# Padding rows dropped at the scatter, scatters of one expert made independent, and the last batch's routing woven in differently

## The chip, the cores and the metric

The kernel runs on one core of a Trainium2 chip. The metric is the device time of one execution in microseconds; the median of three timed runs is given. The core has five engines that run side by side, each in its own order: PE (matrix products), DVE (vectors), ACT (activation functions and copies), POOL (further element-wise work, and here all indirect DMAs), and SP (which here only issues DMAs). They wait for one another through semaphores. DMAs move data between device memory and the on-chip memory.

## The reference, cut to what matters

Two layers act on 4 x 32 x 32 positions of 256 channels, which are 4096 tokens in 4 batches. Layer 0 is a convolution with a state-space scan; layer 1 is an attention and then a mixture of 16 experts. The change concerns the experts:

```python
logits = jnp.einsum('bsd,de->bse', x, gate_w) + gate_b
probs = jax.nn.softmax(logits, axis=-1)
top_probs, top_idx = jax.lax.top_k(probs, 2)
top_probs = top_probs / jnp.sum(top_probs, axis=-1, keepdims=True)
dispatch = jnp.sum(jax.nn.one_hot(top_idx, n_experts, dtype=x.dtype) * top_probs[..., None], axis=-2)
h1 = jnp.einsum('bsd,edh->bseh', x, w1)
h2 = jnp.einsum('bsd,edh->bseh', x, w2)
hidden = jax.nn.silu(h1) * h2
expert_out = jnp.einsum('bseh,eho->bseo', hidden, w3)
return jnp.einsum('bseo,bse->bso', expert_out, dispatch)
```

Every token goes to two of 16 experts, and the two weighted results are added to the token's row `t`, which holds the attention's output. There are 8192 (token, expert) pairs. The input of the experts is the layer-normalised row.

## The kernel before, in words

**Stages.** The scan of layer 0 fills the first 2690 us. The attention of the four batches follows (loop `for o in range(NB)`, line 1817), with the routing of batch `z = o - 1` woven into that of batch `o`. Then comes the expert stage (`blocks_of`, line 2091). The order within an engine is that of the program text (`tc.manual_schedule()`).

**Blocks.** The pairs are sorted by expert into blocks of `BS` = 128 rows. Each expert has `FIX` = 3 fixed blocks; number `s * NE + e` is the s-th of expert e. Pairs that don't fit go to extra blocks, whose expert is known only at run time: `NFULL` = 25 of them always run, further ones only under `tc.If`. That makes 8 + 40 + 25 = 73 blocks: `soon` are the first blocks of experts 0 to 7 (filled from batches 0 to 2 alone), `fixed` are the other 40 fixed ones, and `more` the 25 extra ones.

**One block.** `fetch_rows` (1801) gathers 128 rows of `xd`, the normalised tokens in DRAM, by an indirect DMA on POOL's queue (`src` holds the row numbers, `xb` the rows). `turn_rows` (2037) transposes them on PE into `px`, and ACT copies that to `xT`. `hidden` (2054), called twice a block, forms half of both hidden products on PE (`p12`), the silu on ACT (`s`) and the product on DVE (`hT`). `result` (2073) multiplies by `w3` on PE into `pf`. `put_result` (2082) weighs the result on DVE (`yb`, four buffers) and adds it to the output by an indirect DMA on POOL's queue:

```python
        nc.gpsimd.indirect_dma_start(
            of[:, :], bass.IndirectOffsetOnAxis(dst[:, c : c + 1], 0), yb, None,
            compute_op=ALU.add,
        )
```

All these scatters write the same DRAM tensor, so each waits for the one before it to land.

**Padding.** A block that isn't full has padding rows. They gather the zero row 4096 of `xd`, and add zeros to rows of `out`. [...]padding is sent to tokens that are not in the block. `nonmembers`, `count_them`, `place_them` and `list_them` (1664 to 1696) list 128 such tokens per expert (`table`); `one_block` and `targets` (1770 to 1784), and the end of `more_rows` (2241 to 2270), turn it into the target rows `dst`.

**Order of the stage.** `blocks_of` walks the list `todo`. In step i it gathers ahead (`look_ahead`: four blocks beyond i, six `xb` buffers), computes the first half of block i, the second half of the result of block i - 1 with its scatter, loads weights ahead (`load_ahead`, on SP's queue), transposes block i + 1, and computes the second half of block i. `more` blocks are spread one by one among the fixed ones. Weights of fixed and extra blocks live in separate pairs of buffers (`wp` and `spare`; the names in the profile are `w` and `m`).

**Routing of the last batch.** The routing of batch 3 and the lists of the later blocks depend on the end of the attention. They are a generator (`rest_of_routing`, `spare_rows`, `more_places`, `more_rows`), cut by `yield` into steps. `on_with(beside, 3)` runs three steps after each half block while i < 8, and one step after that. PE steps among them: `turn_e` (transposes), `gates` (gate product), `turn_g`, the counts `pc` (1574), the lists `pf_r` (1652), the extra blocks' experts (2183) and lists (2228).

Of the kernel before, what the change touches and what calls it, by code (L numbers as in the profile page):

```python
# [33 lines left out]
def conv_ssm_attn_moe_kernel(ctx: ExitStack, tc: tile.TileContext, a: dict, out: bass.AP):  # L34
# [1149 lines left out]
    names = l1.tile([P, 2], F32, name="names")  # L1184
    names_h = l1.tile([P, 2], BF16, name="names_h")
    apart = l1.tile([P, 2, NE], F32, name="apart")
    rank = l1.tile([P, 2, NE], F32, name="rank")
    table = l1.tile([P, NE], F32, name="table")
# [17 lines left out]
    def constants(first):  # L1206
# [6 lines left out]
        if first:  # L1213
# [8 lines left out]
            count(names, 2, 0, P, 1)  # L1222
            count(part_pk, 2, 1, 1, 2)
            count(block_p, 1, 0, 1, 1)
        else:
# [8 lines left out]
            nc.vector.tensor_copy(names_h, names)  # L1234
# [293 lines left out]
    def route(b):  # L1528
# [42 lines left out]
        yield  # L1571
        flat = hot2.rearrange("p e g -> p (e g)")
# [60 lines left out]
        nc.vector.tensor_tensor(  # L1633
# [15 lines left out]
        pf = ps_c.tile([P, 2, NFIX], F32, name="pf_r", tag="po")  # L1649
        for k in range(2):  # L1650
            for i in range(NT):
                nc.tensor.matmul(
                    pf.rearrange("p s n -> p (s n)"), qh[:, k, b * NT + i, :],
                    code[:, k * NT + i, :2, :].rearrange("p s n -> p (s n)"),
                    start=(k + i == 0), stop=(k == 1 and i == NT - 1),
                )
# [7 lines left out]
    def nonmembers():  # L1664
        nc.gpsimd.tensor_tensor(apart, hot_all[:, 0, :2, :], hot_all[:, 1, :2, :], ALU.add)
        nc.gpsimd.tensor_scalar(apart, apart, -1.0, 1.0, ALU.mult, ALU.add)

    def count_them():
        pa = ps_c.tile([P, 2, NE], F32, name="pa", tag="po")
        nc.tensor.matmul(pa[:, 0, :], before, apart[:, 0, :], start=True, stop=True)  # L1670
        nc.tensor.matmul(pa[:, 1, :], before, apart[:, 1, :], start=True, stop=False)
        nc.tensor.matmul(pa[:, 1, :], every, apart[:, 0, :], start=False, stop=True)
        nc.scalar.copy(rank, pa)

    def place_them():
        nc.gpsimd.tensor_scalar(apart, apart, -4.0 * P, 4.0 * P, ALU.mult, ALU.add)
        nc.gpsimd.tensor_tensor(rank, rank, apart, ALU.add)
        at = batch[0]["at"] = att.tile(
            [P, 2, NE, BS], BF16, name="at_rank", tag="xh", bufs=2
        )  # L1680
        for g in range(2):
            for e in range(NE):
                nc.gpsimd.tensor_scalar(  # L1683
                    at[:, g, e, :], places_f, rank[:, g, e : e + 1], 1.0,
                    ALU.is_equal, ALU.mult,
                )

    def list_them():
        pt = ps_c.tile([P, NE], F32, name="pt_r", tag="po")
        for e in range(NE):  # L1690
            for g in range(2):
                nc.tensor.matmul(
                    pt[:, e : e + 1], batch[0]["at"][:, g, e, :], names_h[:, g : g + 1],
                    start=(g == 0), stop=(g == 1),
                )
        nc.scalar.copy(table, pt)

    def on_with(steps, n):
        for _ in range(n):
            next(steps, None)  # L1700
# [33 lines left out]
    dst = late.tile([P, NBLK], I32, name="dst")  # L1734
# [6 lines left out]
    move = late.tile([P, NBLK], F32, name="move")  # L1741
    other = late.tile([P, NE], F32, name="other")
    full = late.tile([P, NE], F32, name="full")
# [26 lines left out]
    def targets(lo, hi, move):  # L1770

        cs = slice(lo, hi)
        nc.vector.scalar_tensor_tensor(
            move, move, -1.0 * NB * L, none[:, cs], ALU.add, ALU.mult
        )
        nc.vector.tensor_tensor(dst[:, cs], token[:, cs], move, ALU.add)

    def one_block(lo, hi, held):

        cs = slice(lo, hi)  # L1780
        nc.vector.tensor_scalar(full[:, cs], held[:, cs], float(BS), None, ALU.is_ge)
        nc.vector.tensor_tensor(other[:, cs], token[:, cs], table[:, cs], ALU.subtract)
        nc.vector.tensor_tensor(other[:, cs], other[:, cs], full[:, cs], ALU.mult)
        nc.vector.tensor_tensor(other[:, cs], other[:, cs], table[:, cs], ALU.add)

# [3 lines left out]
    weights = {}  # L1789

# [10 lines left out]
    def fetch_rows(key):  # L1801
# [3 lines left out]
        if c < 3:  # L1805
            t = sm.tile(
                [P, C + 2], F32, name="xb_s", tag="qk" if c else "junk", bufs=2 if c else 1
            )
        else:
            t = on_b["ffn"].tile([P, C + 2], F32, name="xb", bufs=6)  # L1810
# [6 lines left out]
    for o in range(NB):  # L1817
# [26 lines left out]
        if o == 2:  # L1844
            nonmembers()
        if o == 3:
            place_them()
            first_weights("w1")
            first_weights("w3")
        v_out(o, 0)  # L1850
# [75 lines left out]
        if o == 2:  # L1926
            count_them()
        if o == 3:
            list_them()
# [12 lines left out]
        if n is None:  # L1942
            root(batch[o], "ln3", HT, NT)
            expert_in(o, 1)
            choices(0, SOON)
            one_block(0, SOON, counts[NB - 2])
            nc.vector.tensor_copy(move[:, :SOON], other[:, :SOON])
            targets(0, SOON, move[:, :SOON])
# [13 lines left out]
    low = rt.tile([P, NBLK], F32, name="low")  # L1962
    bh = rt.tile([P, 2 * NTA], BF16, name="bh")
    places_of = rt.tile([P, NE], F32, name="places_of")
    places_to = rt.tile([P, NE], F32, name="places_to")
    spare = (
        l1.tile([P, 2, CK, HID], F32, name="m0", tag="tb0"),
        l1.tile([P, 2, CK, HID], F32, name="m1", tag="tb1"),
        l1.tile([P, 2, HK, C], F32, name="m2", tag="tb2"),
    )  # L1970
# [6 lines left out]
    def parts_of(at):  # L1977

        return [
            (name, a["L1_ffn_" + name][at].rearrange(shape, p=P))  # L1980
            for name, shape in (
                ("w1", "o (k p) h -> p (o k) h"),
                ("w2", "o (k p) h -> p (o k) h"),
                ("w3", "o (k p) c -> p (o k) c"),
            )
        ]

    def load(key, at):

        for name, src_ap in parts_of(at):  # L1990
            t = wp.tile([P, HK, C] if name == "w3" else [P, CK, HID], F32, name=name)
            nc.sync.dma_start(out=t, in_=src_ap)
            weights[name, key] = t

    def load_spare(key, at):

        n = weights["spare"] = weights.get("spare", -1) + 1
        for name, src_ap in parts_of(at):
            t = spare[2][:, n % 2] if name == "w3" else spare[n % 2][:, int(name == "w2")]
# [5 lines left out]
    def fetch_weights(todo, j, gone):  # L2005
# [5 lines left out]
        elif c < SOON:  # L2011
            if c == 0:
                return True
            home, last, at = "spare" if (c - 1) % 4 > 1 else "wp", j, slice(e, e + 1)
# [67 lines left out]
    def put_result(key):  # L2082
# [3 lines left out]
        nc.gpsimd.indirect_dma_start(  # L2086
            of[:, :], bass.IndirectOffsetOnAxis(dst[:, c : c + 1], 0), yb, None,
            compute_op=ALU.add,
        )

    def blocks_of(todo, beside=(), fast=0, fetched=0):
# [20 lines left out]
        look_ahead(0, AHEAD)  # L2112
        turn_rows(todo[0])
        for i in range(n + 1):
            if i < n:
                look_ahead(i, AHEAD + 1)
                hidden(todo[i], 0)
            on_with(beside, 3 if i < fast else 1)
# [11 lines left out]
            on_with(beside, 3 if i < fast else 1)  # L2130
        on_with(beside, 99)

    def rest_of_routing():

        o = NB - 1
        turn_e(o, 0)
        yield
        gates(o, 0)
        turn_e(o, 1)
        yield  # L2140
        gates(o, 1)
        yield
        turn_g(o)
        yield
# [6 lines left out]
    def spare_rows():  # L2151

        choices(SOON, NFIX)
        yield
        one_block(SOON, NE, counts[-1])
        nc.vector.tensor_copy(
            move[:, :NFIX].rearrange("p (s e) -> p s e", e=NE), over_middle(other, FIX)
        )
        targets(SOON, NFIX, move[:, SOON:NFIX])
# [44 lines left out]
    def more_rows(lo, hi):  # L2204
# [36 lines left out]
        both = rt.tile([P, 2 * NE], F32, name="both_r")  # L2241
        nc.vector.tensor_copy(both[:, :NE], places_of)
        nc.vector.tensor_copy(both[:, NE:], places_to)
        pst = one()
        nc.tensor.transpose(pst[:NE, :P], both[:, :NE], ident)
        nc.tensor.transpose(pst[:NE, P : 2 * P], both[:, NE:], ident)
        nc.tensor.transpose(pst[:NE, 2 * P : 3 * P], other, ident)
        st = rt.tile([NE, 3 * P], F32, name="st_r")
        nc.scalar.copy(st, pst[:NE, : 3 * P])
        yield  # L2250
        opens = rt.tile([NE, 2, n], F32, name="opens", tag=f"opens{n}")
        bl = blocks[:NE, lo - NFIX : hi - NFIX]
        for i in range(2):
            nc.vector.tensor_scalar(
                opens[:, i, :], bl, st[:, i * P : i * P + 1], None, ALU.is_ge
            )
        nc.vector.tensor_tensor(
            opens[:, 0, :], opens[:, 0, :], opens[:, 1, :], ALU.subtract
        )
        ptab = one()  # L2260
        nc.tensor.matmul(
            ptab[:, :n], st[:, 2 * P :], opens[:, 0, :], start=True, stop=True
        )
        mv = move[:, lo:hi]
        nc.vector.tensor_scalar(
            mv, blocks[:, lo - NFIX : hi - NFIX], places_to[:, NE - 1 :], block_p,
            ALU.is_ge, ALU.mult,
        )
        nc.vector.tensor_tensor(mv, mv, ptab[:, :n], ALU.add)
# [61 lines left out]
```

## Time and profile before

| | |
|---|---|
| median of three timed runs | 3435.76 us (3435.47 to 3437.72) |
| the profiled execution | 3419.33 us, span 3417.6 us |
| PE / DVE / ACT / POOL busy | 93% / 85% / 79% / 80% of the span |
| last product on PE ends | 3396.9 us |
| first row transpose of the expert stage | 2938.2 us |
| mean bandwidth of the last 570 us | 178 GB/s |

Times in the profile count from the start of the span, in microseconds. "Busy" of PE includes time in which its pipeline is filled but slow. In a timeline, a row gives start, length, engine, line and operation, written tile and read tiles, and in brackets how long the engine stood idle before it and which event ended that. A row of waits reads: who waited for whom, total, times, longest. An indirect DMA's row on POOL is only the issuing of its descriptors; the data lands later. Shares of the whole span are set by the scan; what the change is worth is read from the last 480 us.

### The profile page before, as it was taken

What the parts mean: (1) busy time and instruction counts of PE and PEld (TensorE: products, weight loads), DVE (VectorE), ACT (ScalarE), POOL (GpSimd) and SP (SyncE); (2) the same over time, 40 slices, a digit from 0 to 9 for tenths busy, and PEclk for the clock granted to TensorE, in tenths of its full rate; (3) what the DMA queues carried; (4) which work ended last, traced back from release to release, by engine and by line L of the source; (5) the groups of instructions that cost most, each with busy time, mean ns of one, the idle gap of its engine ahead of it and who ended that gap; (6) DMA issues with size and microseconds to landing.
All of it is one profiled execution on the core that took longest, in us unless ns stands there. A gap on an engine that the chain in (4) does not pass through costs nothing. (4 is left out here: it accounts for less than half of the span.)

```text
span 3417.6 us, 62769 instructions
## 1 busy us (share of the span) xinstructions
PE 3175.0 (93%) x23450; PEld 2754.6 (81%) x23450; DVE 2889.6 (85%) x3462; ACT 2716.9 (79%) x4624; POOL 2731.8 (80%) x1176
## 2 busy tenths in 40 slices
PE   7899999999999999999999999989999888799997
PEld 4588988988898988889988888778777666689896
DVE  5699999999999999999999999999999677532222
ACT  1699999999999999999999999999999554221111
POOL 0489998999999989999998999999999535234443
PEclk9999999999999999999999999999999999899998
DMA  3542223224232322233323224222122201567774
GB/s 104 153 67 65 68 68 68 69 70 69 65 80 67 74 70 71 66 57 81 72 72 68 68 65 76 55 62 67 54 66 64 77 31 56 182 167 226 228 230 113
DMA packets 423837, 301.94 MB, mean 88 GB/s; under 512 B 223922, under 2 KB 329394, under 8 KB 423523
## 3 DMA queue, kind: packets, MB, share of 16 engines
q1 hardware_dynamic: 397202, 274.25, 31.0%
q0 software_dynamic: 14016, 19.22, 3.1%
q10 hardware_dynamic: 12304, 4.37, 0.5%
q8 instruction: 187, 3.06, 0.4%
q14 instruction: 128, 1.04, 0.1%
HBM read 262.34 MB, written 34.87 MB: 87 GB/s over the span
## 5 line engine op out<-in xcount | busy, mean ns | idle before, releaser
L961 POOL TENSOR_TENSOR h<-h,cb_n 128x2048 f32<-128x2048 f32 x512 | 2148.8, 4209 | 127.9 <-DVE h L954 85.5
L928 ACT ACTIVATE da<-dt,l_conv_a_log_sb 128x512 f32<-128x512 f32 x2048 | 1437.8, 714 | 20.7 <-DVE h L954 19.7
L908 ACT ACTIVATE bx<-dtxT,proj 128x512 f32<-128x512 f32 x1748 | 1246.5, 713 | 28.4 <-DVE dtxT L600 16.2
L975 PE MATMUL y<-ident,h 128*128 128x128 f32 x8192 | 1235.6, 274 | 9.5 <-POOL h L961 6.6
L954 DVE TENSOR_TENSOR_SCAN h<-da,last,ps 128x512 f32<-128x512 f32 x1024 | 1217.9, 1261 | 6.8 <-PE ps L940 1.6
L954 DVE TENSOR_TENSOR_SCAN h<-da,ps 128x512 f32<-128x512 f32 x1024 | 1169.9, 1202 | 31.3 <-ACT da L928 9.1
L940 PE MATMUL ps<-ident,bx 128*128 128x128 f32 x6992 | 1117.4, 275 | 41.2 <-DVE h L954 28.5
L975 PEld LDWEIGHTS y<-ident,h 128*128 128x128 f32 x8192 | 978.3, 141 | 100.3 <-issue 20.3
L940 PEld LDWEIGHTS ps<-ident,bx 128*128 128x128 f32 x6992 | 818.8, 141 | 100.5 <-DVE h L954 79.4
L2086 POOL DMA_INDIRECT out_dram<-yb,dst x73 | 115.8, 1586 | 257.1 <-DMA out_dram<-yb,dst 124.8
L2069 DVE TENSOR_TENSOR hT<-s,p 128x256 f32<-128x256 f32 x146 | 61.4, 420 | 304.6 <-ACT s L2068 294.9
L940 PE MATMUL ps<-ident,bxp 128*128 128x128 f32 x800 | 236.8, 296 | 50.0 <-DVE h L954 37.8
L2068 ACT ACTIVATE s<-p 128x256 f32<-128x256 f32 x146 | 55.9, 383 | 273.7 <-PE p L2062 260.9
L413 PE MATMUL bg<-pad,dgc 128*128 128x256 f32 x864 | 258.1, 380 | 0.9 <-DMA dgc<-diags 0.9
L940 PEld LDWEIGHTS ps<-ident,bxp 128*128 128x128 f32 x800 | 111.9, 140 | 133.3 <-DVE h L954 79.1
L935 PE MATMUL ps<-dgb,dtxT 128*128 128x128 f32 x800 | 171.0, 296 | 20.8 <-DMA dgb<-diag_b 10.2
L919 POOL TENSOR_SCALAR bxp<-dtxT,proj 128x512 f32<-128x512 f32 x200 | 142.2, 711 | 57.7 <-DVE dtxT L600 57.7
L2062 PE MATMUL p<-xT,w 128*128 128x128 f32 x1440 | 177.5, 277 | 0.5 <-ACT xT L2042 0.5
L2062 PEld LDWEIGHTS p<-xT,w 128*128 128x128 f32 x1440 | 172.8, 193 | 3.2 <-ACT xT L2042 0.9
L935 PEld LDWEIGHTS ps<-dgb,dtxT 128*128 128x128 f32 x800 | 120.5, 190 | 48.1 <-DVE h L954 35.3
L413 PEld LDWEIGHTS bg<-pad,dgc 128*128 128x128 f32 x864 | 130.5, 191 | 1.1 <-DMA dgc<-diags 1.1
L2062 PE MATMUL p<-xT,m 128*128 128x128 f32 x896 | 111.4, 278 | 0.0
(379 smaller groups left out, 2694.1 us busy)
## 6 DMA issues: line engine op xcount, KB each, us to landing
cb_n<-cd SPq DMA_DIRECT2D x512, 256.0 KB
m<-in_L_ffn_w_dram SPq DMA_DIRECT2D x84, 512.0 KB
w<-in_L_ffn_w_dram SPq DMA_DIRECT2D x63, 512.0 KB
dgc<-diags SPq DMA_DIRECT2D x84, 192.0 KB
diag_b<-zero SPq DMA_DIRECT2D x2, 4096.0 KB
dgb<-diag_b SPq DMA_DIRECT2D x100, 64.0 KB
last<-h SPq DMA_DIRECT2D x256, 2.0 KB
xd<-xe SPq DMA_DIRECT2D x8, 512.0 KB
```

Source lines behind the costliest of these rows:

```text
L413: nc.tensor.matmul(made["bg"].rearrange("p (h w) -> p h w", w=WW)[:, blk(c, deep), :], made["dgc", m * 3 + i][:, j, :], pads[m][:, at : at ...
L908: nc.scalar.activation(t, made["dtxT", u][:, j, :], AF.Copy, scale=made["proj", u][:, j, R + n : R + n + 1])
L919: nc.gpsimd.tensor_scalar(t, made["dtxT", u][:, 0, :], made["proj", u][:, 0, R + n : R + n + 1], 1.0, ALU.mult, ALU.mult,)
L928: nc.scalar.activation(t, made["dt", u][:, m, :], AF.Exp, scale=A[:, m, n : n + 1])
L935: nc.tensor.matmul(t[:, blk(j, P)], made["dtxT", steps[s][0]][:, j, blk(m, P)], made["dgb", s], start=True, stop=True,)
L940: nc.tensor.transpose(t[:, blk(j, P)], made["bx", s, j][:, blk(m, P)], ident)
L954: nc.vector.tensor_tensor_scan(h[:, m, 1:], made.pop(("da", s, m)), made.pop(("dbx", s, m)), 0.0 if seg == 0 else last[b][:, n, m : m + 1] ...
L961: nc.gpsimd.tensor_tensor(h[:, :, :BANK], h[:, :, 1:], over_middle(made["c", s], DK), ALU.mult)
L975: nc.tensor.matmul(made["y", u][j][:, blk(m, P)], made["h", s][:, m, blk(j, P)], ident, is_transpose=True, start=n == 0 and m == 0, stop=n ...
L2062: nc.tensor.matmul(p12[:, j, s, :], w_of(w, key)[:, ck, blk(h + j, P)], on_b["xT", key][:, ck, :], start=(ck == 0), stop=(ck == CK - 1),)
L2069: nc.vector.tensor_tensor(on_b["hT", key][:, h : h + 2, :], s, p12[:, :, 1, :], ALU.mult)
L2086: nc.gpsimd.indirect_dma_start(of[:, :], bass.IndirectOffsetOnAxis(dst[:, c : c + 1], 0), yb, None, compute_op=ALU.add,)
```

## The change

1. The scatter uses `src`, the gather's own row numbers, with a bound of 4095: padding (row 4096) is dropped, and the lists that found other targets for it (`nonmembers`, `count_them`, `place_them`, `list_them`, `one_block`, `targets`, the last third of `more_rows`) are gone. A `memset` of one element on POOL stands ahead of each scatter.
2. Scatters of fixed blocks of one expert that follow one another don't wait for one another; they wait for those of the blocks before (`flight`). An extra block is a flight of its own. The list `todo` puts an expert's fixed blocks side by side, then up to two extra blocks; the last two experts are followed by none.
3. Gathers run six blocks beyond i (seven with block i), with nine `xb` buffers.
4. Weights of the second and third block are loaded from the start of the last batch's attention (`next_weights`), ahead of the stage.
5. The first `turn_e` and `gates` of batch 3 stand ahead of the first row transpose. Up to four steps of routing run per half block, but a step that ends with `yield "rest"`, put ahead of PE steps, ends the turn. The product of `code` by `groups` moves from DVE to POOL for batches 0 to 2.

```diff
-        nc.vector.tensor_tensor(
+        (nc.vector if b == NB - 1 else nc.gpsimd).tensor_tensor(
             code[:, :, 0, :], ih,
...
         pf = ps_c.tile([P, 2, NFIX], F32, name="pf_r", tag="po")
+        yield "rest"
...
     def on_with(steps, n):
         for _ in range(n):
-            next(steps, None)
+            if next(steps, None) == "rest" and n < 40:
+                break
...
+    def next_weights():
+        on_b["spare"] = (
+            l1.tile([P, 2, CK, HID], F32, name="m0", tag="tb0"),
+            l1.tile([P, 2, CK, HID], F32, name="m1", tag="tb1"),
+            l1.tile([P, 2, HK, C], F32, name="m2", tag="tb2"),
+        )
+        for c, e in soon[1:3]:
+            load_spare((c, e), slice(e, e + 1))
...
         if o == 3:
-            place_them()
             first_weights("w1")
             first_weights("w3")
+            next_weights()
...
-        nc.gpsimd.indirect_dma_start(
-            of[:, :], bass.IndirectOffsetOnAxis(dst[:, c : c + 1], 0), yb, None,
-            compute_op=ALU.add,
-        )
+        nc.gpsimd.memset(tick, 0.0)
+        s = nc.gpsimd.indirect_dma_start(
+            of[:, :], bass.IndirectOffsetOnAxis(src[:, c : c + 1], 0), yb, None,
+            bounds_check=NB * L - 1, oob_is_err=False, compute_op=ALU.add,
+        ).ins
+        e = key[1]
+        if e is None or not flight["now"] or flight["of"] != e:
+            flight["past"], flight["now"], flight["of"] = flight["now"], [], e
+        for one in flight["now"]:
+            tc.declare_no_dep(s, one, reason="rows of one expert's fixed blocks differ")
+        for one in flight["past"]:
+            tc.add_manual_dep(s, one.name, ...)
+        flight["now"].append(s)
...
         look_ahead(0, AHEAD)
+        if fast:
+            turn_e(NB - 1, 0)
+            gates(NB - 1, 0)
         turn_rows(todo[0])
         for i in range(n + 1):
             if i < n:
-                look_ahead(i, AHEAD + 1)
+                look_ahead(i, 7)
                 hidden(todo[i], 0)
-            on_with(beside, 3 if i < fast else 1)
+            on_with(beside, 4 if i < fast else 1)
...
-    for i, key in enumerate(fixed):
-        todo.append(key)
-        if i >= LEAD:
-            upto = min(NFULL, NFULL * (i + 1 - LEAD) // (len(fixed) - LEAD - TAIL))
-            todo += more[given:upto]
-            given = upto
+    for e in (*range(SOON, NE), *range(SOON)):
+        todo += [k for k in fixed if k[1] == e]
+        n = len({k[1] for k in todo if k not in soon})
+        upto = min(NFULL, max(0, NFULL * (n - 1) // (NE - 3)))
+        todo += more[given:upto]
+        given = upto
```

## The prediction, made before the changed kernel ran

> **What bounds the kernel now.** I read the forty slices first, then busy time by stretch, then the waits and the engine timelines of the last 480 us. The change leaves the long scan (up to about 2690 us) alone; the expert stage runs from the first row transpose (2938.2 us) to the end.
>
> ```profile
> 2938.20:3015.05 76.85, 60.83 (x457) 52.34 (x457) 40.41 (x151) 21.98 (x46) 20.93 (x17) 0.93 0.73 221
> 3015.05:3396.90 381.85, 364.28 (x2733) 343.08 (x2732) 101.76 (x328) 73.62 (x194) 159.22 (x123) 1.00 0.72 205
> ```
>
> Columns: stretch, length, busy time (instructions) of PE, PEld, DVE, ACT, POOL, then PE clock, DMA share, GB/s. In the second stretch PE is busy 95%. The chain of waits shows its undisturbed pace: pairs of hidden products start at 3018.12, 3023.64, 3029.16, 3034.68, so a block of 128 rows takes 5.52 us. From 3015.05 on 65 blocks remain: 65 x 5.52 = 358.8, plus 0.9 for the last half result, is 359.7; it took 381.8. So 22.1 us are lost here.
>
> ```profile
> POOL out_dram L2086 <- DMA out_dram<-yb,dst: 124.8, 37, 5.7
> PE px L2040 <- DMA xb<-xd,src: 17.5, 14, 3.4
> ```
>
> Every scatter waits until the one before it has landed (124.8 us over 37 waits), the next gather is queued behind it on POOL, and PE waits for gathered rows 14 times, 17.5 us. The rest of the 22.1 is PE running slow after such a wait (below).
>
> ```profile
> 3125.59 1.59 POOL L2086 DMA_INDIRECT out_dram<-yb,dst  x1 [4.41 <-DMA out_dram<-yb,dst]
> 3127.48 0.99 POOL L1811 DMA_INDIRECT xb<-xd,src  x1 [0.30 <-PE p L2062]
> 3132.87 1.59 POOL L2086 DMA_INDIRECT out_dram<-yb,dst  x1 [4.40 <-DMA out_dram<-yb,dst]
> ...
> 3397.63 1.55 POOL L2086 DMA_INDIRECT out_dram<-yb,dst  x1 [3.03 <-DVE yb L2084]
> 3402.15 1.55 POOL L2086 DMA_INDIRECT out_dram<-yb,dst  x1 [2.97 <-DMA out_dram<-yb,dst]
> 3406.75 1.55 POOL L2086 DMA_INDIRECT out_dram<-yb,dst  x1 [3.04 <-DMA out_dram<-yb,dst]
> ```
>
> One link is 7.28 us here. From the scatter at 3092.88 to that at 3388.47 there are 51 links in 295.6 us: 5.80 each, 0.28 more than PE needs. Scatters therefore fall behind, PE is held to their pace, and when PE ends at 3396.9 three scatters are left; the last starts 9.85 us after PE's end.
>
> ```profile
> 2963.18 0.49 PE L1574 MATMUL pc<-hot,every_t 128*128 128x128 f32 x2 [2.07 <-DVE hot L1568]
> ...
> 2975.85 0.82 PE L1652 MATMUL pf_r<-code,qh 128*128 128x96 bf16 x8 [2.70 <-DVE qh L1644]
> ...
> 2987.36 0.27 PE L2183 MATMUL one<-ident,ef 128*1 128x128 f32 x1 [3.23 <-DVE ef L2181]
> ```
>
> In the first stretch the routing of the last batch is woven into the first blocks and PE stands before its steps until DVE is done. All such idle times between 2963 and 3015 sum to 15.4 us.
>
> **The change part by part.**
>
> *Independent scatters.* Today 5 of 5 links are serial. Now the three (for the first eight experts two) fixed blocks of an expert wait only for the flight before them; the 25 extra blocks stay serial. A link between independent scatters costs POOL 1.59 + 0.99 + 2 x 0.30 of gaps = 3.2 us. A round of three fixed and two extra blocks has three serial links: 3 x 5.80 + 2 x 3.2 = 23.8 us against PE's 5 x 5.52 = 27.6. A round of two and two: 3 x 5.80 + 3.2 = 20.6 against 22.1. Both are below PE, so the scatters stop setting the pace. Of the 22.1 us I take back 20; 2 stay because the second kind of round has only 1.5 us to spare.
>
> Here a rule speaks against the change. The Trainium skill ("DMA: Bandwidth & Descriptors", Anatomy of one DMA — SWDGE (gpsimd) path) fits such a DMA as 2.0 us plus bytes over 436 GB/s: for 128 KB 2.3 us, so by estimate a link of 1.59 + 2.3 = 3.9 us, below PE's 5.52: the chain could not bind, and this part would give nothing. The trace says 4.9 us from issue to landing (3.7 to 8.0) and 5.80 a link, beside weight loads and accumulating into DRAM. I go by the trace.
>
> *Tail.* Without backlog the last scatter starts about 1.3 us after PE's end (yb 0.48, two gaps of 0.3, the memset) instead of 9.85: 8.5 us. The list now ends with two experts of two fixed blocks and no extra ones. I take 7.5, for a small remaining backlog (bounds 3.5 and 8.6).
>
> *Gathers seven ahead, nine buffers.* This prices itself only if scatters still lag: a gather then tolerates two blocks (11 us) more. What is late next is yb: four buffers, so DVE holds block i until scatter i-4 has landed, about 17 us of slack.
>
> *Bound check and memset.* Neither is in the trace. Padding rows no longer write, and 73 x 128 - 8192 = 1152 of 9344 rows are padding, so landing can be shorter (at most 12%, 0.6 us a link); a comparison per row can lengthen the 1.59 us of POOL. I take zero, as the nearest row is the scatter itself; POOL has 5.52 - 3.2 = 2.3 us a block to hide the growth. Without that cover each us over it costs one us a block. The memset of one element is nearest to L1676 (128x32, 0.23 us): 0.2 us a block in the same cover.
>
> *Order of blocks and weights.* Still 49 weight sets. In the stretch 3100:3260 the queue q1 moved 28.05 MB in 52.8% of 160 us, 332 GB/s: 1.57 MB a set is 4.7 us; q0 took 22.9% for 53 indirect DMAs, 1.4 us a block. A three-and-two round needs 3 x 4.7 + 5 x 1.4 = 21.1 of 27.6 us, a two-and-two round 19.7 of 22.1, 89%. Weights are asked for up to three blocks ahead, so I cost this at nothing; it is the next limit.
>
> *Two weight sets earlier.* Six loads of 512 KB go onto SP's queue behind the w1/w3 loads (issued at 2873.4) and ahead of the row stores at 2888.4 and the weights at 2905.5. The w3 slots use batch 2's tile, read until 2888.4 (xe), so SP waits there; six issues took 3.8 us at 2939.8, so the stores slip by about 2 to 4 us. Their first reader, the gather, starts at 2933.3, and 3.1 MB need 9.5 us on queues that were 17% busy: hidden. If not, gathers slip by as much. PE does not wait for weights in the first blocks today: gain zero.
>
> *Routing split.* The first transposes and gate product of batch 3 (2943.01 to 2946.87, 3.86 us of PE) move ahead of the first row transpose, where PE idles 7.46 us for gathered rows. Their three ACT copies stand behind xe, which ends at 2935.9, so the row transpose slips to about 2938.9: net gain 3.1. Four steps per half block, broken off before PE steps, give DVE at least half a block (2.76 us) for each. But DVE is the floor: it is busy 39.33 us in 2953.6:3015.0, about 1.5 us of that disappears (targets), and PE needs about 46. In bursts hT queues behind them on DVE, so I leave 6 of the 15.4 us (bounds 3 and 15): gain 9.4. Three transposes and the table product go: 0.6.
>
> *Ahead of the stage.* The padding list costs POOL 25.4 us (L1683). The chain names it, yet nothing needs it in time: its product on PE starts only at 2926.9 and POOL idles 22 us after it. So 25.4 us of POOL are worth nothing. PE loses 0.6 and 0.8 us of small products. The pf_r product of batch 2 stood 1.92 and 2.36 us before DVE; its split returns some. The product `code` of batches 0 to 2 moves from DVE (0.95) to POOL; by 0.73 us for 256 and 1.29 for 512 elements I take 1.9, beside DVE's 2.4 us of qh. Together 2.0 (bounds 0 and 5.6).
>
> **Sum.** 20 + 7.5 + 3.1 + 9.4 + 0.6 + 2.0 = 42.6. The profiled execution took 3419.3 (span 3417.6), so 3376.7. The median of the timed runs is 16.4 us above it; I assume the same distance: 3435.8 - 42.6 = 3393.2, 1.2% faster. The bounds together give 31 to 55 us.
>
> PE's clock belongs to this. After 3.36 us idle at 3241.5 sixteen products took 3.33 us instead of 1.95; after 2.7 us at 2975.9 they took 2.78. The skill ("TensorE: Matmul & The Clock Gate", Part 1) halves the clock after one idle window of about 3.4 us; by it only one of the 14 waits would be punished, 1.5 us, where the loss past the 17.5 us is 4.6. I use the 4.6.
>
> **The rivals.**
> 1. *The serial links still bind* (0.14): experts' borders and extra blocks, with landing at 6.9 us in the denser second half: 3 x 6.9 + 3.2 = 23.9 against 22.1, 1.8 us x 6 rounds = 11 us, partly covered, with the backlog kept. Against it: the 5.80 mean already holds the loads. Gain 42.6 - 12 - 7.5 = 23: 3412.7.
> 2. *Routing only moves its stall* (0.10): four steps in a burst delay hT, and PE stops for DVE instead. 42.6 - 9.4 - 3.1 = 30: 3405.7.
> 3. *The scatters stay serial after all* (0.06), because a queue's semaphore or a remaining dependence orders them. Then only routing and start remain: 15 us, 3420.7. For it: completion is told per DMA.
> 4. *Slower* (0.05): the bound check makes the scatter's POOL time the pace. It decides from 1.59 + 2.3 = 3.9 us. To lose the 42.6 and 7 more over 65 blocks takes 0.76 us a block, a scatter of about 4.6 us: 3443. Against it: 1.59 us for 128 rows is 12 ns a row, and the check would have to add 24.
>
> **How the numbers follow.** The forecast has 0.65. Range 3378 to 3415: the forecast's bounds (3381 to 3405) with rivals 1 and 2; a little below for shorter landings. About 0.2% (7 us) is what a measurement of this kernel can tell from no change. Faster 0.93 (forecast and rivals 1 to 3, less a little), same 0.02, slower 0.05.
>
> **What would show it.** Right: POOL's wait on landing falls from 124.8 to below 60 us; PE's wait for gathered rows below 4 us; the last scatter starts within 5 us of PE's end; scatters of one expert stand 5.5 us apart without waits; idle time before L1574, L1652 and L2183 below 6 us; transposes of batch 3 before the first px. Wrong: scatters above 2.5 us on POOL, waits of PE on w or m (weights), waits of yb on out_dram, or a pace over 5.6 us in the second half.

## The result, and the profile after

The changed kernel takes 3387.51 us (median of 4 runs, 3385.20 to 3389.96), against 3435.61 us for the kernel before in the same comparison (4 runs, 3434.11 to 3437.72): the ratio is 0.986, with a 95% interval from 0.9843 to 0.9877. It is 48.1 us faster; 42.6 us were forecast. The profiled execution took 3389.96 us (span 3387.8).

The two profiled spans lie only 29.8 us apart, because the unchanged scan ended at different times. I therefore count from a mark that no edit touches: the first product into `po_l` (line 1308 before, 1301 after), with which the end of layer 0 begins. It starts at 2684.3 us in the profile before and at 2700.8 after. From it to the end of the span are 733.3 us before and 687.0 after: 46.3 us of gain in the part that was changed.

Busy time by stretch, kernel after. The first stretch is from the first hidden product of the expert stage to the first transpose of block 9, the second from there to the last product on PE (columns as in the prediction):

```profile
2951.14:3018.73 67.59, 58.15 (x458) 52.36 (x459) 38.92 (x139) 19.48 (x42) 23.42 (x27) 0.95 0.66 188
3018.73:3376.10 357.37, 357.27 (x2713) 340.10 (x2711) 100.84 (x325) 73.39 (x193) 165.59 (x188) 1.00 0.75 218
```

In the second stretch PE is busy all but 0.1 us. The first transposes of blocks 9 and 72 are 347.8 us apart, 63 blocks of 5.52 us each: the pace at which nothing but PE itself is waited for. The clock is full, and the DMA share rose only from 0.72 to 0.75.

The same row of the waits as before, and POOL's timeline in the place where one link took 7.28 us before:

```profile
POOL out_dram L2033 <- DMA out_dram<-yb,src: 51.8, 13, 6.7
```

```profile
3135.69 1.59 POOL L2033 DMA_INDIRECT out_dram<-yb,src  x1 [4.27 <-DVE yb L2030]
3137.59 0.99 POOL L1786 DMA_INDIRECT xb<-xd,src  x1 [0.30 <-issue]
3138.88 1.59 POOL L2033 DMA_INDIRECT out_dram<-yb,src  x1 [0.22 <-issue]
3140.77 0.99 POOL L1786 DMA_INDIRECT xb<-xd,src  x1 [0.30 <-PE px L1986]
3142.07 1.60 POOL L2033 DMA_INDIRECT out_dram<-yb,src  x1 [0.23 <-issue]
...
3376.87 1.56 POOL L2033 DMA_INDIRECT out_dram<-yb,src  x1 [2.25 <-DVE yb L2030]
```

The row of waits that end on a landing fell from 124.8 us to 51.8. It names only part of these waits, before and after. The first scatter shown is said to have waited for `yb`, but its `yb` had been ready since 3129.83; what came last was the landing of the scatter before, at 3134.88. So I also count from the timelines how long POOL stood idle before a scatter whose `yb` was ready (stretches under 0.5 us left out): 199.5 us ahead of 64 scatters before, 124.6 us ahead of 40 after. The distance from a ready `yb` to its scatter grew to 19.7 us before; now it never passes 7.9 and is back at 0.3 for the last five blocks. PE has no wait for gathered rows left among its waits.

Three scatters start 3.19 us apart, as costed (3.2): whenever the last scatter of the flight before has landed, POOL catches up on the ones that lag behind it. The last row is the tail. PE ends at 3376.07 and the last scatter starts 0.8 us later, where it was 9.85.

PE's timeline in the first stretch, rows with idle time before them and one slow row:

```profile
2946.77 3.42 PE L1510 MATMUL pgT<-xeT,l_ffn_gate_w_sb 128*16 128x512 f32 x4 [3.33 <-ACT xeT L1281]
...
2988.28 0.27 PE L2135 MATMUL one<-ident,ef 128*1 128x128 f32 x1 [2.11 <-DVE ef L2133]
...
2996.36 0.36 PE L2180 MATMUL one<-code,qh 128*128 128x50 bf16 x8 [1.67 <-ACT code L2175]
...
2998.05 3.65 PE L2008 MATMUL p<-xT,m 128*128 128x128 f32 x16
...
3003.46 0.36 PE L2180 MATMUL one<-code,qh 128*128 128x50 bf16 x8 [1.55 <-ACT code L2175]
```

The routing still stops PE, at other steps than before: ahead of the extra blocks' experts (2135) and of their lists (2180). Idle time ahead of the routing's steps is 7.6 us, where it was 15.4. Another 1.8 us, ahead of the hidden products at 2978.58, are a wait for ACT's copy of the rows (`xT`); 9.35 us in all from 2978 to 3005. After one such group sixteen products take 3.65 us instead of 1.95. The first gate product now waits 3.33 us for ACT's copy and then runs slowly.

### The profile page after: what moved, and what is told of

Its sections match the earlier page's. It is cut to its first block, busy times and chain, and to the rows that moved or that the text cites. A ratio compares the mean times of both kernels' runs of the same rounds, so it can differ in the third digit from the quotient of the medians.

```text
span 3387.8 us, 62750 instructions
## 1 busy us (share of the span) xinstructions
PE 3172.2 (94%) x23407; PEld 2753.3 (81%) x23407; DVE 2886.9 (85%) x3435; ACT 2717.3 (80%) x4621; POOL 2718.4 (80%) x1215
## 3 DMA queue, kind: packets, MB, share of 16 engines
q0 software_dynamic: 14016, 18.05, 2.8%
## 5 line engine op out<-in xcount | busy, mean ns | idle before, releaser
L908 ACT ACTIVATE bx<-dtxT,proj 128x512 f32<-128x512 f32 x1748 | 1246.9, 714 | 29.9 <-DVE dtxT L600 16.4
L954 DVE TENSOR_TENSOR_SCAN h<-da,ps 128x512 f32<-128x512 f32 x1024 | 1169.8, 1201 | 41.8 <-DMA last<-h 16.8
L2033 POOL DMA_INDIRECT out_dram<-yb,src x73 | 116.0, 1589 | 212.3 <-DVE yb L2030 82.2
```

The source lines that it names most:

```text
L908: nc.scalar.activation(t, made["dtxT", u][:, j, :], AF.Copy, scale=made["proj", u][:, j, R + n : R + n + 1])
L954: nc.vector.tensor_tensor_scan(h[:, m, 1:], made.pop(("da", s, m)), made.pop(("dbx", s, m)), 0.0 if seg == 0 else last[b][:, n, m : m + 1] ...
L2033: s = nc.gpsimd.indirect_dma_start(of[:, :], bass.IndirectOffsetOnAxis(src[:, c : c + 1], 0), yb, None, bounds_check=NB * L - 1, oob_is_er ...
```

## The experiments

Every kernel was timed beside the kernel before on the same chip, and "gain" is the distance between those two medians. The ratios' intervals are about plus or minus 0.2%, 5 to 8 us. The traces, counted from the mark, separate some of the smaller effects better, though each is one execution. How far they repeat: e2 and the changed kernel end 687.6 and 687.0 us after the mark, the two runs of e4 727.8 and 730.3, and the two of the kernel before 733.3 and 742.1.

| kernel | median, us | gain, us | ratio (95%) | mark to end, us |
|---|---|---|---|---|
| the change | 3387.51 | 48.1 | 0.986 (0.9843 to 0.9877) | 687.0 |
| e1_serial | 3411.83 | 21.7 | 0.9931 (0.9909 to 0.9952) | 713.2 |
| e2_gather5 | 3384.66 | 48.9 | 0.9851 (0.9831 to 0.9872) | 687.6 |
| e6_serial_gather5 | 3412.08 | 21.5 | 0.993 (0.991 to 0.9949) | 714.8 |
| e3_three_steps | 3385.10 | 48.4 | 0.9856 (0.9834 to 0.9878) | 690.8 |
| e4_bound_only | 3418.71 | 15.8 | 0.9954 (0.9938 to 0.9969) | 727.8 |
| e5_old_order | 3392.44 | 42.1 | 0.9872 (0.985 to 0.9894) | 693.8 |
| e7_code_dve | 3385.80 | 48.7 | 0.9855 (0.9833 to 0.9877) | 688.6 |
| e10_gates_after | 3389.12 | 45.4 | 0.9868 (0.9845 to 0.989) | 691.9 |
| e9_late_weights | 3388.24 | 42.7 | 0.9874 (0.9856 to 0.9891) | 691.5 |
| e8_more_rest | 3377.61 | 53.3 | 0.9846 (0.9829 to 0.9864) | 679.4 |

### Scatters and gathers: e1, e2, e6

**e1_serial** is the change without the declaration that scatters of one expert's fixed blocks are independent:

```diff
-        for one in flight["now"]:
-            tc.declare_no_dep(s, one, reason="rows of one expert's fixed blocks differ")
```

> The changed kernel, but every scatter again waits for the one before it; block order, gathers seven ahead, nine buffers, bound and routing stay. Theory A (the serial scatter chain set the pace and left the backlog; its independence is what returned the 22 us in the steady part and the 9 us of the tail): 5.8 us a link against 5.52, so 18 to 20 us of lag, of which the four yb buffers hide about 3 blocks at most, all paid at the tail: 18 to 31 us slower than the changed kernel, 3406 to 3418 us; PE waits through yb or hT, not for xb. Theory B (the deeper gathers freed PE, and the scatters' lag is mostly harmless): at most 10 us slower, all in the tail.

**e2_gather5** is the change with the gathers' depth of before; **e6_serial_gather5** makes both edits.

```diff
-            t = on_b["ffn"].tile([P, C + 2], F32, name="xb", bufs=9)
+            t = on_b["ffn"].tile([P, C + 2], F32, name="xb", bufs=6)
...
-                look_ahead(i, 7)
+                look_ahead(i, AHEAD + 1)
```

> The changed kernel with gathers four blocks beyond i and six xb buffers, as before; scatters of one expert stay independent. Theory A: 0 to 4 us slower (single gathers behind a serial link of an extra block), under 4 us of PE waiting for xb. Theory B: 15 to 20 us slower, and PE waits for xb again about as often as before.

> The changed kernel with serial scatters and gathers only four blocks beyond i. Theory A: about as slow as with serial scatters alone, 22 to 32 us over the changed kernel (3410 to 3420), with PE waiting for xb instead of yb: the depth only moves where PE waits. Theory B: clearly slower than serial scatters alone, by 15 us or more.

Serial scatters cost 26.4 of the 48.1 us of gain, deep gathers or not; the shallow gathers alone cost nothing. In e1's trace the 63 blocks from block 9's transpose to the last one's take 360.6 us, where the change takes 347.8 (63 x 5.52). From the start of the last `yb` it has 24.5 us to the end, where the change has 11.7. These two differences make 25.6 us, about all of the loss. The waits and one row of PE, first of e1, then the waits of e6:

```profile
DVE yb L2030 <- DMA out_dram<-yb,src: 79.1, 22, 6.2
PE pf L2023 <- DVE hT L2015: 10.3, 9, 2.4
```

```profile
3293.46 1.13 PE L2023 MATMUL pf<-w,hT 128*128 128x256 f32 x4 [2.43 <-DVE hT L2015]
```

```profile
POOL out_dram L2033 <- DMA out_dram<-yb,src: 109.8, 32, 6.6
PE px L1986 <- DMA xb<-xd,src: 8.1, 10, 1.9
```

The serial chain binds in both kernels, and the depth of the gathers only chooses where PE feels it. With deep gathers the four `yb` buffers fill first: DVE waits 79.1 us for landings, `hT` is queued behind `yb` on DVE, and PE waits for `hT`, 10.3 us in nine waits. With shallow ones the next gather stands behind the scatter on POOL, and PE waits for rows as it did before the change.

### Order of the blocks: e5

**e5_old_order** is the change with the list of before, which spreads the fixed blocks of an expert and the extra ones:

```diff
-    for e in (*range(SOON, NE), *range(SOON)):
-        todo += [k for k in fixed if k[1] == e]
...
+    for i, key in enumerate(fixed):
+        todo.append(key)
+        if i >= LEAD:
...
```

> The changed kernel with the list of blocks in the order of before, extra blocks spread singly among the fixed ones; scatters of neighbouring fixed blocks of one expert are still independent, gathers seven ahead. Theory A (independence pays only where fixed blocks stand side by side): in the middle nearly every link is serial again at about 5.8 us, so 8 to 14 us of lag build up; the last fixed blocks without extra ones recover part of it: 5 to 15 us slower than the changed kernel, PE waiting through yb. Rival (any independent link is enough): within 3 us of the changed kernel.

The gain falls by 6.0 us, by itself within the two intervals; the trace ends 6.8 us later. Waits of e5:

```profile
POOL out_dram L2033 <- DMA out_dram<-yb,src: 89.1, 29, 5.6
DVE yb L2030 <- DMA out_dram<-yb,src: 15.5, 5, 5.3
```

More links are serial: with `yb` ready, POOL stands idle 151.4 us ahead of 54 scatters, where the change has 124.6 ahead of 40. Sometimes all `yb` buffers are taken. From block 9 to the last one it loses 1.8 us; the last scatter starts 4.2 us after the last `yb` does, where the change has 0.8, and the remaining 1.6 us lie ahead of block 9.

### The bound alone: e4, and the kernel before once more

**e4_bound_only** is the kernel before with the bounded scatter; the lists for padding are gone, and nothing else is changed:

```diff
-            of[:, :], bass.IndirectOffsetOnAxis(dst[:, c : c + 1], 0), yb, None,
-            compute_op=ALU.add,
+            of[:, :], bass.IndirectOffsetOnAxis(src[:, c : c + 1], 0), yb, None,
+            bounds_check=NB * L - 1, oob_is_err=False, compute_op=ALU.add,
```

> The kernel before with only the first part of the change: scatters use src with a bound of 4095, the padding lists (nonmembers to list_them, one_block, targets, the last third of more_rows) are gone; no memset, scatters serial, order, gathers and routing steps as before. Theory A (POOL's 25 us of padding list were nothing's wait; the check itself is free): scatter on POOL still 1.59 us, first gather at most 2 us earlier, 2 to 6 us faster than before in all. Rival (the 6.3 us by which the first gather starts earlier in the changed kernel, counted from the attention's first product, come from the padding list's removal): first gather 4 to 6 us earlier, 7 to 12 us faster than before.

**e4_again** and **b_again** are the same kernel and the kernel before for another profile, since two traces had left open how much of this is chance.

> The kernel before with only the bound check and without the padding lists, profiled once more, since its first profile (727.8 us from the attention's first product to the end) is 5.5 us below the kernel before, but its median 16. Theory A: about 728 again, within 4, and the rest of the difference lies in the scan, which the edit doesn't touch. Rival: the stage with serial scatters varies, and typically takes 718 to 722 here.

> The kernel before, profiled once more. The first profile was 16.4 us shorter than the median of the timed runs. Theory A: that difference lies in the scan, before the attention's first product (2684.3 us there, 2694 to 2704 in the traces of the other kernels): here that product comes at 2690 to 2705, and from it to the end it takes 733 us again, within 4. Rival: the scatter-bound stage itself varies by 10 us and more, and the first profile had a good or bad one.

One group of POOL in e4:

```profile
L2074 POOL DMA_INDIRECT out_dram<-yb,src x73 | 116.0, 1589 | 254.6 <-DVE yb L2072 91.3 <-DMA out_dram<-yb,src 74.4 <-DVE hT L2057 41.1
```

The bound costs POOL nothing: 1589 ns a scatter, against 1586 before. The part is worth more than either expectation made it: 15.8 us timed. Its two traces are of slower executions than that median (3427.23 us, and 3429.80 for e4_again, whose comparison had the kernel before at 3430.92), so they may show less of it. b_again ran in 3436.13 us, as the median does, and explains the distance between the profiled execution before and the median: of its 16.8 us, 8.0 lie ahead of the mark (2692.3 against 2684.3) and 8.8 behind it (742.1 us to the end against 733.3).

The serial chain itself varies from run to run. e4 ended 727.8 and 730.3 us behind the mark, so its stage gains 3.0 to 14.3 us, by which of the two runs of before it is held against. About 3.5 of that stand at the head: the first gather starts 245.5 and 246.2 us after the mark instead of 249.0 and 249.5. After the first gather the rest is less sure: from block 9 to the last block e4 took 367.9 and 366.8 us, before took 369.6 and 374.9. The row of waits on landings is smaller (74.4 us, against 124.8 and 95.7), but with `yb` ready POOL stood idle 196.9 and 202.5 us in e4 and 199.5 and 208.1 before. That the 1152 rows less to write make landings shorter is therefore not shown.

### The routing: e3, e10, e7, e8

**e3_three_steps** takes back the four steps and the early end of a turn:

```diff
-            if next(steps, None) == "rest" and n < 40:
-                break
+            next(steps, None)
...
-            on_with(beside, 4 if i < fast else 1)
+            on_with(beside, 3 if i < fast else 1)
```

> The changed kernel with three routing steps per half block and no early end of a turn at the PE steps. Theory A (splitting at the PE steps is what shortened PE's waits for DVE): idle time of PE before routing steps back from 9 to about 15 us, and the wait before pf_r of batch 2 back: 5 to 10 us slower, 3393 to 3398. Rival (DVE's work is the floor and the split only moves the wait): within 3 us of the changed kernel.

The way in which the turns are cut is worth nothing that shows: the gain is 48.4 us. From block 0's transpose to block 9's it takes 70.4 us, the change 68.6, and e1, e2, e5 and e7, whose routing is cut as in the change, 68.8 to 70.7. In those kernels and the change PE is idle for about the same time in these blocks, 9.7 to 10.1 us; the spread goes with the granted clock (0.95 in the change, 0.91 in e1, where the first sixteen products took 3.79 us instead of 2.05). In e3 PE is idle for 10.1 us as well. The cut took waits ahead of the routing's steps (9.7 us in e3, 7.6 in the change) and gave most of it back as waits for `xT` (0.5 and 2.2). PE's rows of e3 stand before the same steps:

```profile
2995.09 0.27 PE L2134 MATMUL one<-ident,ef 128*1 128x128 f32 x1 [2.20 <-DVE ef L2132]
...
3008.40 0.36 PE L2179 MATMUL one<-code,qh 128*128 128x50 bf16 x8 [1.62 <-ACT code L2174]
```

**e10_gates_after** puts batch 3's first transposes and gate product back among the steps:

```diff
-        if fast:
-            turn_e(NB - 1, 0)
-            gates(NB - 1, 0)
...
+        turn_e(o, 0)
+        yield
+        gates(o, 0)
```

> The changed kernel with the first transposes and gate product of batch 3 after the first block's first half, as steps of the routing, as before. Theory A (they filled PE's wait for gathered rows): first row transpose 0.5 to 2 us earlier, the stretch from it to the tenth 4 us longer, 2 to 4 us slower in all. Rival (they stand in the way, since PE waits 3.3 us for their ACT copies and runs them at a slow clock): 0 to 3 us faster.

```profile
2942.61 0.66 PE L1986 MATMUL px<-ident,xb_s 128*128 128x128 f32 x2 [7.39 <-DMA xb_s<-xd,src]
```

PE stands idle for 7.39 us again before the first transpose. The first transpose comes 2.1 us earlier after the mark than in the change, but the nine blocks, which now hold the moved steps, take 75.4 us instead of 68.6: 4.7 us lost, while the timed gain falls by 2.7. Of the 4.7 us, 1.0 stand ahead of the first gather, which the edit doesn't touch. From that gather to block 9 it takes 79.0 us, the change 75.3, e1, e2, e5, e6 and e7 76.3 to 76.6, before 84.5 and e4 85.3. The moved step is thus worth 2.4 to 3.7 us there. PE's idle time in the nine blocks is 9.7 us in e10 and 10.1 in e3, as in the change (9.8), and 15.9 before. Either edit taken back alone leaves it near 10 us; which of them brought it down, or whether either suffices, no run separates.

**e7_code_dve** leaves the product of `code` by `groups` on DVE:

```diff
-        (nc.vector if b == NB - 1 else nc.gpsimd).tensor_tensor(
+        nc.vector.tensor_tensor(
```

> The changed kernel with the product of code by groups on DVE for all batches, as before. Theory A: it explains part of the earlier first gather, 0.95 us of DVE in the tight end of the attention: 0 to 3 us slower. Rival: on DVE it is faster than on POOL (POOL's wait before it, the longer operation), and the changed kernel gets 0 to 3 us faster.

No difference that shows: 48.7 us. Why the move brings nothing stands in DVE's and POOL's timelines of the change:

```profile
2852.34 4.05 DVE L1639 TENSOR_TENSOR qh<-places,qb 128x1024 bf16<-128x1024 bf16 x2
...
2902.57 1.22 DVE L1639 TENSOR_TENSOR qh<-places,qb 128x1024 bf16<-128x1024 bf16 x1
...
2904.04 2.16 DVE L1639 TENSOR_TENSOR qh<-places,qb 128x1024 bf16<-128x1024 bf16 x1
```

```profile
2852.17 1.47 POOL L1628 TENSOR_TENSOR code<-code,groups 128x768 bf16<-128x768 bf16 x1 [6.39 <-DVE code L1623]
...
2902.73 2.39 POOL L1628 TENSOR_TENSOR code<-code,groups 128x768 bf16<-128x768 bf16 x1 [1.96 <-DVE code L1623]
```

and in DVE's of e7:

```profile
2848.45 2.35 DVE L1639 TENSOR_TENSOR qh<-places,qb 128x1024 bf16<-128x1024 bf16 x2
```

For batch 0 POOL's product starts first and takes 1.47 us; DVE's two `qh` take 4.05 us, where e7 needs 2.35. For batch 1 the first `qh` stands first and takes its 1.22 us; POOL's product, begun beside it, takes 2.39, and the second `qh` takes 2.16 and ends 1.08 us after POOL's product does. The two engines took turns. Over the three batches the move takes 2.84 us of products off DVE and lengthens its `qh` by 3.15 (1.70, 0.94 and 0.51), both held against e7. The Trainium skill ("SBUF — State Buffer", Who interferes with whom) says just this of a DVE instruction with two inputs in SBUF and a GpSimd instruction that reads SBUF; the prediction had set the two beside each other.

**e8_more_rest** goes the other way and ends the turn before the PE steps at which the change still waits:

```diff
+        yield "rest"
         pe = one()
...
-                yield
+                yield "rest"
```

> The changed kernel, with the turn also ended before the PE steps that it leaves unsplit: the transpose of the extra blocks' experts, and the eight list products of the extra blocks, which so run one or two per half block. Theory A (what PE still waits for in the routing is these steps: 7 us of idle time and 3.5 us of slow clock after it): 3 to 8 us faster than the changed kernel, those waits below 1 us. Rival (DVE is the floor there, as the three-steps run suggests): within 2 us, PE waits for hT or xT instead.

PE's rows and the busy time of its nine blocks:

```profile
2979.97 0.27 PE L2136 MATMUL one<-ident,ef 128*1 128x128 f32 x1 [0.42 <-DVE ef L2133]
...
2986.83 0.36 PE L2181 MATMUL one<-code,qh 128*128 128x50 bf16 x8 [1.07 <-DVE code L2172]
```

```profile
2941.70:3000.20 58.50, 54.00 (x437) 48.59 (x437) 35.57 (x124) 18.94 (x41) 22.84 (x26) 1.00 0.77 227
```

The waits before 2135 and 2180 fall from 2.11 to 0.42 us and from seven of 0.18 to 1.67 to one of 1.07. The clock stays at 1.00, and the nine blocks take 58.5 us instead of 68.6. Of these 10.1 us, 5.5 are idle time ahead of the routing's steps (7.6 and 2.1) and some 3.5 the slow clock. The last list products now run behind block 9; from there to the last block e8 takes 1.1 us longer. It ends 679.4 us after the mark, 7.6 before the change. It is the fastest kernel run, 3377.61 us. Against the change, which was timed in another comparison, the gain is 5.2 us larger; the intervals of the two ratios overlap, so the trace carries this rather than the timing.

### Weights early: e9

**e9_late_weights** loads the second and third block's weights inside the stage, as before:

```diff
-        for c, e in soon[1:3]:
-            load_spare((c, e), slice(e, e + 1))
...
```

> The changed kernel with the weights of the second and third block loaded at the start of the expert stage instead of during the last batch's attention. Theory A (the earlier loads are worth nothing, since 5 us a set are hidden under the routing steps): within 2 us of the changed kernel, no wait of PE on w or m. Rival (with PE faster in the first blocks the weights are late): PE waits 2 to 6 us on w or m, as much slower.

```profile
PE p L2004 <- DMA w<-in_L_ffn_w_dram: 1.1, 1, 1.1
```

```profile
2994.41 3.76 PE L2004 MATMUL p<-xT,m 128*128 128x128 f32 x16
```

The gain falls by 5.4 us, within what the two intervals leave open, and the trace ends 4.5 us later. The one wait for weights stands at 3092.17, far behind the first blocks, and e6, which loads early, has one there too (2.3 us, at 3094.57). In the first nine blocks PE waits for no weights. They take 71.3 us, 2.7 more than in the change but only 0.6 more than in e1, e2, e5 and e6. Two groups of products run slowly (3.76 and 3.04 us) after waits ahead of the lists. That the early loads are worth anything is not shown.

Dropping the `memset` ahead of the scatter was not tried. In the trace its 73 instructions take 160 ns each, 11.7 us in all, on an engine that waits for `yb` far longer.

## Why the prediction was right, point by point

**Steady part: 20 us forecast, 21.8 found.** From block 8's first product, 65 blocks and the last half result should take 359.7 us and took 360.0 (3016.08 to 3376.07), where before took 381.8. The mechanism was the forecast one, and e1 shows it by its absence. By the skill's rule for one DMA, which the prediction had weighed against the trace's link, e1 should have lost nothing. It lost 26.4 us, so the trace was the better guide. Rivals 1 and 3 fell with the same trace.

The link itself was miscounted. From 3092.88 to 3388.47 there are 50 scatters, so 49 links of 6.03 us and not 51 of 5.80: 0.51 us more than PE needs. Rounds then cost 24.5 us against 27.6 and 21.3 against 22.1, which is still below PE, but with 0.8 us to spare instead of 1.5. The 22.1 us lost before were read from PE's own time and stand. Nor do the 124.8 us name all waits for landings (199.5, see above).

**Tail: 7.5 forecast, 8.9 found** (20.7 us from PE's end to the end of the span before, 11.8 after). I had left a backlog of about 1 us that isn't there.

**Gathers seven ahead: worth nothing while scatters keep up.** e2 confirms it. The prediction also named `yb` as what would be late next, and e1 shows that.

**Head of the stage and routing: 15.1 forecast (3.1 + 9.4 + 0.6 + 2.0), 15.5 found.** Block 8's first product starts 315.3 us after the mark instead of 330.75. The sum fits, its terms do not; that their errors cancel is luck.
- The term "I leave 6 of the 15.4 us" was too good: 7.6 us are left ahead of the routing's steps, 1.8 came as a wait for `xT`, and some 3.5 us of slow clock go with them. e3 shows that the cutting into turns, to which I gave the whole 9.4, gives nothing measurable beside the moved step. The extra blocks' experts and lists kept their waits, as they have no turn's end ahead of them; e8 gives them one and takes 10.1 us out of the nine blocks. So rival 2 was right in its mechanism for these steps, without costing what it had reckoned.
- The transposes moved ahead were forecast at 3.1 us net; e10 says 2.4 to 3.7 in the traces from the first gather on, 2.7 timed.
- "25.4 us of POOL are worth nothing" was wrong. The first gather starts 6.3 us earlier after the mark (242.7 against 249.0), and e4, which drops the lists without touching the routing's order, has about 3.5 us of it. The chain of waits that had named this list was right, at least in part. How the list delays the gather is not settled: one wait of 0.62 us on DVE ends with it. With the earlier gather, the first row transpose came 4.6 us earlier, not about as early as before.
- "PE does not wait for weights in the first blocks: gain zero" is not contradicted: without the early loads PE waits for none there either. How much of the 4.5 us that e9 loses in its trace is owed to the loads, no run shows.

**Bound check: zero taken on POOL's time, and right** (1.589 us); rival 4 fell. The bound with the lists was undervalued all the same, see e4.

**The distance between profile and median.** I assumed that the 16.4 us were the same before and after. They were not: the profiled execution after lies 2.4 us above its median. b_again places half of the distance in the scan and half in the stage, so the trace of before showed its serial stage in a rather quick execution. Against b_again's stage the gain would be 55.1 us (742.1 - 687.0), of which 8.5 are lost again since the mark comes later after the change (2700.8 against 2692.3). The mark lay between 2684.3 and 2703.7 us in the fourteen profiles, the two of the kernel before being the first and the third. Why it varies, and whether the changes move it at all, stays open. That the quick stage (8.8 us) and the later mark (8.5 us) nearly cancel in the forecast is luck.

**The listed signs.** The row of waits on landings is 51.8 us (below 60), though by the count with `yb` ready it fell only from 199.5 to 124.6; PE's wait for rows is gone, the last scatter stands 0.8 us after PE's end, no idle time stands before the counts `pc`, and 0.62 us before `pf_r`. Scatters of one expert were to stand 5.5 us apart; without waits they stand 3.19 apart, since they catch up. Missed is the idle time before the extra blocks' experts: 2.11 us, below the bound of 6 by itself, but hardly less than the 3.23 of before.

## What to carry to other kernels

When a queue of dependent DMAs is slower than the engine that feeds it by some 9% (6.03 us against 5.52 here), every link counts: take the cost of a link from start to start in the trace, and free only as many links as bring a round below the engine's pace. Deeper buffers ahead of such a queue move the place of the wait and not its length. When a helper's work is woven into a busy engine's stream, look for the step that has its wait still, one row at a time, and put the pause ahead of that one; in this case the cut at other steps brought nothing that shows.

## What the runs showed of the hardware that was not expected

- Bounded scatters that drop rows cost no more time to issue (1.589 us for 128 rows) and move less: queue q0, that of the indirect DMAs, carried 18.05 MB instead of 19.22 in as many packets.
- A scatter that waits for the one before starts 0.79 us after that one's landing (median), and a landing comes 4.9 us after the issue (median), both in the kernel before.
- Scatters in flight together did not land later than single ones: of the landings that the change's trace holds, 34 that overlap another have a median of 4.8 us, the other 36 of 5.6. The median over all, 5.3 us, lies above the 4.9 of before, but e4_again has 5.2 with every scatter serial.
- POOL and DVE products of two bf16 operands took turns instead of overlapping. Begun first, POOL's took 1.47 us and DVE's two 4.05 instead of 2.35; begun second, POOL's took 2.39.
- PE's clock fell after several short waits, none above 1.7 us: 2.6 us of idle time in the 3.9 us from 2994.1 to 2998.0, then 3.65 us for what takes 1.95 at full clock. Columns as before; the third number from the end is the granted clock:

```profile
2994.10:2998.00 3.90, 1.28 (x32) 1.27 (x31) 3.33 (x12) 2.11 (x6) 2.75 (x3) 1.00 0.54 126
2998.05:3001.70 3.65, 3.65 (x29) 3.59 (x25) 0.37 (x1) 0.46 (x1) 0.00 (x0) 0.53 0.16 40
```

- One longer wait need not do the same. In the kernel before, PE stood 3.23 us before 2987.36, the clock stayed at 1.00 to 2990.0, and sixteen products took 2.02 us. In the change a wait of 3.33 us ahead of the first gate product nearly doubled its time (3.42 us, the second takes 1.89).
